# An additive-attention stage on one NeuronCore: from key tile 14 on, the steps follow a table of times, with one exponential for two groups and a fourth numerators' bank

## The chip, the core and the metric

The kernel is one program on one core of a Trainium2 chip. TensorE (PE) multiplies matrices into PSUM, which has eight banks of 128 partitions x 512 float32. VectorE (DVE), ScalarE (ACT) and GpSimd (POOL) work on tiles of 128 partitions; each engine runs its own queue in order, and engines wait for each other by semaphores. The metric is the device time of one execution in microseconds (us), the median of several runs.

## The reference, cut to what matters

The whole model is a selective-scan block (layer 0), then this attention, then a recurrence (layer 1). Only the attention is touched:

```python
t = _to_tokens(x)                      # 4 images, 4096 tokens, 128 channels, float32
t = t + _L1_attn_ref(_ln_t(t), ...)    # _ln_t: layer norm over the channels
...
q = jnp.einsum('bld,ud->blu', x, Wt)   # U = 32
k = jnp.einsum('bld,ud->blu', x, Wx)
beta = jnp.tanh(q[:, :, None, :] + k[:, None, :, :] + bh)
alpha = jnp.einsum('bsju,u->bsj', beta, Wa[:, 0]) + ba[0]
alpha = jnp.tanh(alpha)
alpha = jax.nn.softmax(alpha, axis=-1)
c_r = jnp.einsum('bsj,bjd->bsd', alpha, x)
```

There is a `beta` of 32 values for each of 4 x 4096 x 4096 pairs of query and key, so the tanh can't be formed one by one. The kernel writes a sum of six (or five) tanh terms as one fraction: numerator and denominator are each a sum of 64 (or 32) products of an exponential of the key and an exponential of the query, and such a sum is one matrix product.

## The kernel before

`_bounded` runs three stages: `_layer0`, then `_rational` (this attention), then `_chunked` (the recurrence). `_rational` works through 32 blocks: four images `b`, each with eight blocks `s` of 512 queries. For one block the keys come in 32 tiles `jt` of 128, so `A[:, jt, :]` (128 keys x 512 queries) is the score of one step. `F` holds the keys' exponentials, `E` the queries', `cE` the queries' with the weights of the numerators.

The 32 units are split into three groups: "A" (two fractions, each a product over 64 rows, on partitions 0 to 63 and 64 to 127), "B1" (two over 32 rows, partitions 0 to 31 and 32 to 63) and "B2" (two over 32 rows, partitions 64 to 95 and 96 to 127). A step does for each group:

- `lower`: two matmuls into a tile `pd` of two PSUM banks, the denominators (line 1212). `pd` has two buffers.
- `upper`: two matmuls into two tiles `pn` of one bank each, the numerators (line 1212 too). `pn` has three buffers; one more bank, `ct`, is for the weighted sum and for small products.
- `inverse`: 1/denominator as Ln (line 1231, PSUM to SBUF) and Exp with scale -1 (line 1232, in place), both on ACT over 128x1024.
- `times`: two DVE multiplications of the inverse by the numerators (line 1227), which free the `pn` banks.

POOL adds the three groups: B1 to A on line 1346, B2 to A on line 1333 (below a1 and a2). DVE then adds the two halves into `A[:, jt, :]` on line 1343 (below f); f is the one DVE operation of a step with both inputs in SBUF. The results `ra` have three buffers, `rb` four.

A stage is scheduled by hand: each engine's queue has the order in which the Python code issues. In one step of the loop (line 1323) PE does dA(j), nB2(j-1), dB1(j), nA(j), dB2(j), nB1(j), where d are lower and n upper products; ACT does Ln and Exp of A, then of B1, then of B2; DVE does xB2(j-1), xA(j), xB1(j), f(j-1), where x is `times`; POOL does a2(j-1), a1(j).

After the 32 steps comes the tail (line 1380): ACT runs tanh and exp over `A` in four parts. Meanwhile DVE does step 0 of the next block with reciprocals of its own (`direct`, lines 1239 and 1240) and f of that step (line 1396); before that it forms the next `cE` (`weigh`, line 1200), on which the first numerators of the next block wait. PE sums `ct` over key tiles 0 to 19 in the tail (`weighted`, line 1357).

The rest is put between the steps of the next block, by the dictionary `between`, after the step whose number is the key: the last twelve `weighted` at 2 to 13; at `CLOSE_AT` the closing of the block before: `ct` copied to SBUF (1249), one matmul for the denominator (1253), four reciprocals of 128x128 that read it in PSUM (1258), one matmul for the numerator (1262), a multiplication (1263), POOL's addition to `xr` (1264) and the store; at `NORM_AT` the layer norm of 512 tokens of the next image (centre, square, rate, scale; lines 1149 to 1164), in the blocks of the first three images; at `QUERIES_AT` the two matmuls, exponentials and maxima for the next block's `E` (line 1194). At the first block of an image eight `turn` (transposes into `xT`) are put in too.

Of the kernel before, what the change touches and what calls it, by code (L numbers as in the profile page):

```python
# [15 lines left out]
P = 128  # L16
B = 4
# [25 lines left out]
CLOSE_AT = (14, 16, 17, 18, 19, 20, 22)  # L43
NORM_AT = (15, 17, 19, 20)
QUERIES_AT = (24, 26)
# [1000 lines left out]
def _rational(ctx, tc, k, x1, x2, top, Wt, Wx, bh, Wa, ba):  # L1046
# [15 lines left out]
    rb = ctx.enter_context(tc.tile_pool(name="nrb", bufs=4))  # L1062
    psD = ctx.enter_context(tc.tile_pool(name="npsD", bufs=2, space=PSUM))
    psN = ctx.enter_context(tc.tile_pool(name="npsN", bufs=3, space=PSUM))
    psW = ctx.enter_context(tc.tile_pool(name="npsW", bufs=1, space=PSUM))
# [6 lines left out]

    def pn():
        return psN.tile([P, QB], F32, name="pn", tag="pn")

    def pw():
        return psW.tile([P, QB], F32, name="ct", tag="ct")
# [65 lines left out]
    def norm_steps(xn, cols, alloc):  # L1143
# [10 lines left out]
        def square():  # L1154
            held["sq"] = rb.tile([P, CH], F32, name="sq", tag="rb")[:, 0:n]
            nc.scalar.activation(held["sq"], xc, AF.Square)
# [37 lines left out]
    def queries(E, xn, s, i):  # L1194
        exponent(pw(), w_q, xn[:, s * QB : (s + 1) * QB], i, E[:, i, :])
# [33 lines left out]
    def inverse(d, pool, tag):  # L1229
        r = pool.tile([P, 2, QB], F32, name=tag, tag=tag)  # L1230
        nc.scalar.activation(r, d, AF.Ln, scale=LOWER)  # L1231
        nc.scalar.activation(r, r, AF.Exp, scale=-1.0)  # L1232
        return r

    def direct(d, ns, pool, tag):

        r = pool.tile([P, 2, QB], F32, name=tag, tag=tag)
# [3 lines left out]
        return r  # L1241

    def closing(b, s, ct, xr, parts):
# [7 lines left out]
        def denominators():  # L1251
            held["den"] = pw()
            nc.tensor.matmul(held["den"], den_w, held["ct"], start=True, stop=True)
            held["rec"] = one.tile([P, QB], F32, name="rec")

        def invert(i):
            cols = slice(i * QB // parts, (i + 1) * QB // parts)
            nc.vector.reciprocal(held["rec"][:, cols], held["den"][:, cols])

        def end():  # L1260
            num = pw()
# [32 lines left out]
    between = {}  # L1294
    for c in range(1, nq):
        for i in range(2):
            between.setdefault(2 * c - 2 + i, []).append(lambda c=c, i=i, xn=xn: keys(F, xn, c, pw(), i))
    for c in range(nq):
        between.setdefault(16 + c, []).append(lambda c=c, xn=xn: turn(xT, xn, c))
    for b in range(B):  # L1300
        upcoming = None
        for s in range(nq):
# [4 lines left out]
            if b + 1 < B:  # L1307
# [4 lines left out]
                for at, go in zip(NORM_AT, norm_steps(upcoming, blocks[s], pn)):  # L1312
                    between.setdefault(at, []).append(go)
            if more:
                E_next = two.tile([P, 2, QB], F32, name="E")
                of = upcoming if turned else xn
                for i in range(2):
                    between.setdefault(QUERIES_AT[i], []).append(
                        lambda i=i, s=s, of=of, E_next=E_next: queries(E_next, of, (s + 1) % nq, i)
                    )  # L1320
            ln_exp()
            late = None
            for jt in range(start, JT + 1):
                if jt < JT:
                    dA = lower("A", F, jt, E) if jt > start else first[0]
                if late is not None:
                    pj, rA_, rB2_ = late
                    nB2 = upper("B2", F, pj, cE)
                if jt < JT:
                    dB1 = lower("B1", F, jt, E) if jt > start else first[1]  # L1330
                if late is not None:
                    times(rB2_, nB2)
                    nc.gpsimd.tensor_tensor(rA_, rA_, rB2_, ALU.add)  # L1333
                if jt < JT:
                    nA = upper("A", F, jt, cE)
                    rA = inverse(dA, ra, "ra")
                    times(rA, nA)
                    dB2 = lower("B2", F, jt, E)
                    nB1 = upper("B1", F, jt, cE)
# [322 lines left out]
```

## Time and profile before

| what | us |
|---|---|
| median of 3 runs (from 11648.04 to 11656.42) | 11649.02 |
| the profiled execution's own time | 11654.41 |
| its span, first to last instruction | 11652.7 |
| PE busy, of the span | 10307.6 (88%) |
| ACT busy | 9520.9 (82%) |
| DVE busy | 8997.6 (77%) |
| POOL busy | 8625.1 (74%) |
| the attention's groups: Ln of `rb` (1231), x1986 | 2007.6 |
| Exp of `rb` (1232), x1986 | 2099.6 |
| Ln of `ra` (1231), x993 | 1008.7 |
| Exp of `ra` (1232), x993 | 1049.6 |

The page divides the span into 40 slices, and gives for each engine a digit of busy tenths. The attention takes the slices from the fourteenth on, up to nearly the last. The page's groups give the count and the mean time of one instruction; the timeline gives each instruction's start, its duration, and in brackets how long its engine had been idle before it and what ended that. Instructions of one kind that follow each other are merged in the timeline (x2, x4). A float32 matmul is two passes, each with its weight load.

### The profile page before, as it was taken

Reading aid. Unit: us, or ns where it says so; the run is one execution under the profiler, and the core shown is the slowest. Engines: PE = TensorE matmul, PEld = TensorE weight load, DVE = VectorE, ACT = ScalarE, POOL = GpSimd, SP = SyncE. Lnnn points to the kernel's source line nnn. Section 1 sums busy time; section 2 is a strip of 40 time slices with the busy share of each in tenths; the row PEclk is TensorE's granted clock in tenths of the full one; section 3 lists DMA queues with packets and bytes.
Section 4 is the critical chain, followed back from the end, with each engine's and each line's share of the span. In section 5 each row is a group of like instructions: output and inputs, shape, how many; then the busy total and the mean of one; then the engine's idle time right before and its main releaser. Section 6 shows DMA issues by size and latency. Waiting matters only on the chain.

```text
span 11652.7 us, 111820 instructions
## 1 busy us (share of the span) xinstructions
PE 10307.6 (88%) x36210; PEld 3184.3 (27%) x36210; DVE 8997.6 (77%) x10066; ACT 9520.9 (82%) x10209; POOL 8625.1 (74%) x3703
## 2 busy tenths in 40 slices
PE   6787787778777699999999999999999999999997
PEld 2121121122111133333333333333333333333334
DVE  4998899889889677777777777777777777777773
ACT  3566556656655599999999999999999999999996
POOL 3999889889889677767766776767677767776773
PEclk8898898889888799999999999999999999999998
DMA  4888778778778300000000000000000000000001
GB/s 118 189 182 194 171 177 193 170 182 190 179 171 186 79 1 3 6 3 3 6 3 3 3 6 3 3 3 6 3 3 3 6 2 3 3 4 3 2 3 60
DMA packets 225332, 737.77 MB, mean 63 GB/s; under 512 B 41104, under 2 KB 41936, under 8 KB 223712
## 3 DMA queue, kind: packets, MB, share of 16 engines
q1 hardware_dynamic: 221760, 729.96, 26.5%
q8 instruction: 286, 4.69, 0.2%
q14 instruction: 310, 2.54, 0.1%
q10 hardware_dynamic: 2976, 0.58, 0.0%
HBM read 612.95 MB, written 117.44 MB: 63 GB/s over the span
## 4 chain that ended last, share of the span: by engine, by line
PE 50%; ACT 9%; DVE 4%; issue 3%; POOL 0%; DMA 0%; DVEq 0%; POOLq 0%; SPq 0%; ACTq 0%
PE pn L1212 26%; PE pd L1212 16%; PE ct L1357 4%; ACT A L1381 3%; ACT A L1382 2%; DVE rb L1227 2%; ACT rb L1231 1%; ACT rb L1232 1%; PE ct L1134 1%; ACT ra L1231 1%; DVE rb L1239 1%; PE vy L1556 0%; DVE A L1343 0%; PE pn L56 0%; PE ct L1262 0%
## 5 line engine op out<-in xcount | busy, mean ns | idle before, releaser
L1212 PE MATMUL pn<-cE,F 32*128 32x512 f32 (+1 forms) x12288 | 4728.8, 650 | 196.6 <-DVE rb L1227 88.5
L1227 DVE TENSOR_TENSOR rb<-rb,pn 128x512 f32<-128x512 f32 x3972 | 2544.5, 682 | 1310.9 <-PE pd L1212 684.9
L1212 PE MATMUL pd<-E,F 32*128 32x512 f32 (+1 forms) x12288 | 3478.0, 648 | 20.9 <-DVE ra L1239 15.7
L1346 POOL TENSOR_TENSOR ra<-ra,rb 128x1024 f32<-128x1024 f32 x993 | 2634.5, 2653 | 957.2 <-DVE rb L1227 956.9
L1333 POOL TENSOR_TENSOR ra<-ra,rb 128x1024 f32<-128x1024 f32 x993 | 2346.8, 2363 | 409.0 <-DVE rb L1227 348.4
L626 POOL TENSOR_TENSOR dBu<-dtdu,bbcc 128x1024 f32<-128x1024 f32 x1024 | 2398.3, 2368 | 216.9 <-DMA dtdu<-ddd 155.5
L1232 ACT ACTIVATE rb<-rb 128x1024 f32<-128x1024 f32 x1986 | 2099.6, 1057 | 62.8
L1212 PEld LDWEIGHTS pn<-cE,F 32*128 32x128 f32 (+1 forms) x12288 | 1418.0, 185 | 2574.8 <-DVE rb L1227 1066.6
L1231 ACT ACTIVATE rb<-pd 128x1024 f32<-128x1024 f32 x1986 | 2007.6, 1011 | 89.9 <-PE pn L1212 75.2
L668 PE MATMUL py<-h,gather 128*32 128x512 f32 x4096 | 1297.9, 699 | 477.3 <-POOL h L651 364.5
L1227 DVE TENSOR_TENSOR ra<-ra,pn 128x512 f32<-128x512 f32 x1986 | 1317.9, 684 | 231.4 <-ACT ra L1232 175.6
L1212 PEld LDWEIGHTS pd<-E,F 32*128 32x128 f32 (+1 forms) x12288 | 931.4, 185 | 1638.5 <-issue 693.7
L621 ACT ACTIVATE pa<-dtdu,a_neg 128x1024 f32<-128x1024 f32 x1024 | 1145.3, 1119 | 53.1 <-DVE h L641 32.1
L651 POOL TENSOR_TENSOR h<-h,bbcc 128x1024 f32<-128x1024 f32 x384 | 912.0, 2375 | 346.2 <-ACT carry L649 338.5
L641 DVE TENSOR_TENSOR_SCAN pa<-pa,carry,dBu 128x1024 f32<-128x1024 f32 x480 | 1124.7, 2343 | 23.1 <-ACT pa L621 11.3
L1232 ACT ACTIVATE ra<-ra 128x1024 f32<-128x1024 f32 x993 | 1049.6, 1057 | 31.4
L1357 PE MATMUL ct<-A,xT 128*128 128x512 f32 x2048 | 1050.9, 641 | 8.2 <-ACT A L1382 8.2
L1231 ACT ACTIVATE ra<-pd 128x1024 f32<-128x1024 f32 x993 | 1008.7, 1016 | 60.0 <-PE pd L1212 26.5
L649 ACT COPY carry<-pa 128x1 f32<-128x1 f32 x640 | 102.4, 160 | 1043.7 <-DVE h L648 1041.9
L1343 DVE TENSOR_TENSOR A<-ra 128x512 f32<-128x512 f32 x993 | 745.0, 750 | 116.3 <-POOL ra L1333 116.0
L648 DVE TENSOR_TENSOR h<-pa,bbcc 128x1024 f32<-128x1024 f32 x640 | 784.1, 1225 | 59.0 <-PE py L668 0.9
L641 DVE TENSOR_TENSOR_SCAN h<-pa,carry,dBu 128x1024 f32<-128x1024 f32 x288 | 675.0, 2344 | 171.1 <-PE py L668 148.2
(291 smaller groups left out, 8731.3 us busy)
## 6 DMA issues: line engine op xcount, KB each, us to landing
bbcc<-bcd SPq DMA_DIRECT2D x1024, 256.0 KB, 6.9
dtdu<-ddd SPq DMA_DIRECT2D x1024, 256.0 KB, 7.1
ddd<-dd SPq DMA_DIRECT2D x64, 1024.0 KB, 5.1
src<-src SPq DMA_DIRECT2D x64, 512.0 KB, 8.3
xs<-in_x_dram SPq DMA_DIRECT2D x16, 512.0 KB, 7.5
src<-xs SPq DMA_DIRECT2D x16, 512.0 KB, 3.0
bcd<-bc SPq DMA_DIRECT2D x64, 128.0 KB, 2.0
src<-xsT SPq DMA_DIRECT2D x16, 512.0 KB, 5.4
```

Of the source, the lines that this page charges most:

```text
L621: nc.scalar.activation(dA, its[m].DT[r][:, 0, :], AF.Exp, scale=a)
L626: nc.gpsimd.tensor_tensor(dBu, its[m].DT[r][:, 1, :], its[m].BC[q][:, 0, :], ALU.mult)
L641: nc.vector.tensor_tensor_scan(to[:, step], dA[:, step], live.pop(("dBu", u))[:, step], 0.0 if m % nch == 0 else its[m - 1].carry[:, col : ...
L651: nc.gpsimd.tensor_tensor(h, h, cc, ALU.mult)
L668: nc.tensor.matmul(it.y[to, c], gather, live["h", v][:, c], start=False, stop=(q == QS - 1))
L1212: nc.tensor.matmul(ps[a], F[lo:hi, i, jt * P : (jt + 1) * P], side[lo:hi, i, :], start=True, stop=True)
L1227: nc.vector.tensor_tensor(r[:, a, :], r[:, a, :], ns[a], ALU.mult)
L1231: nc.scalar.activation(r, d, AF.Ln, scale=LOWER)
L1232: nc.scalar.activation(r, r, AF.Exp, scale=-1.0)
L1333: nc.gpsimd.tensor_tensor(rA_, rA_, rB2_, ALU.add)
L1346: nc.gpsimd.tensor_tensor(rA, rA, rB1, ALU.add)
L1357: nc.tensor.matmul(ct, xT[:, jt, :], A[:, jt, :], start=(jt == 0), stop=(jt == JT - 1))
```

## The change

1. The loop over `jt` is replaced by `steps`, which gives for each tile a list of (time, function). The lists of all tiles and what stood in `between` are sorted by time, and issued in that order. A table says at what time, counted in steps from the tile's own number, each operation stands. Tiles below `LATE` = 14 have a table that gives the old order. Tiles from 14 on have another.
2. From tile 14 on the Ln of B1 and of B2 write the two halves of one tile of 128x2048 and one Exp does both. In the new order ACT does lnA, lnB1, exA, lnB2, exB; PE does nB1(j-1), dB2(j), nB2(j-1), dA(j+1), nA(j), dB1(j+1); DVE does xB1(j-1), f(j-2), xB2(j-1), xA(j); POOL does a1(j-1), a2(j-1).
3. `rb` becomes three buffers of 128x2048 (each has room for B1 and B2 of a step) where there were four of 128x1024.
4. The four single banks are now tiles `pn0` to `pn3`. `pn()` takes them in turn: three of them up to time 13.95, four from there to the end of the steps, where the bank of `ct` has been copied out. `pw()`, which the weighted sum uses, is always `pn3`.
5. The closing moves to the times 13.95 to 18.9. The denominators are copied from PSUM to `rec` in SBUF (one DVE instruction more for each block), and the reciprocals read them there. Its matmuls and those of the queries take a bank by `pn()`.
6. The norm moves from after the steps 15, 17, 19, 20 to the times 19.9, 20.95, 21.95, 23.95; its squares share the buffer of `rec`. The queries stay after step 24 and 26 by their number (24.9 and 26.9), the `weighted` come a step earlier (1.9 to 12.9).

```diff
-CLOSE_AT = (14, 16, 17, 18, 19, 20, 22)
-NORM_AT = (15, 17, 19, 20)
-QUERIES_AT = (24, 26)
+LATE = 14
+CLOSE_AT = (13.95, 15.9, 16.4, 16.9, 17.4, 17.9, 18.9)
+NORM_AT = (19.9, 20.95, 21.95, 23.95)
+QUERIES_AT = (24.9, 26.9)
+EARLY_STEPS = dict(
+    dA=0.00, dB1=0.10, nA=0.20, lnA=0.21, exA=0.22, xA=0.23, dB2=0.30, nB1=0.31, lnB1=0.40, exB1=0.41,
+    xB1=0.42, a1=0.44, lnB2=0.50, exB2=0.51, nB2=1.05, xB2=1.12, a2=1.13, f=1.43,
+)
+LATE_STEPS = dict(
+    dA=-0.44, dB1=-0.23, lnA=-0.12, lnB1=-0.04, exA=0.26, dB2=0.37, lnB2=0.50, nA=0.74, xA=0.81, exB=0.84,
+    nB1=1.11, xB1=1.38, nB2=1.42, xB2=1.49, a1=1.75, a2=1.88, f=2.46,
+)
...
-    rb = ctx.enter_context(tc.tile_pool(name="nrb", bufs=4))
+    rb = ctx.enter_context(tc.tile_pool(name="nrb", bufs=3))
...
-    psN = ctx.enter_context(tc.tile_pool(name="npsN", bufs=3, space=PSUM))
-    psW = ctx.enter_context(tc.tile_pool(name="npsW", bufs=1, space=PSUM))
+    psN = ctx.enter_context(tc.tile_pool(name="npsN", bufs=1, space=PSUM))
...
+    turns = {"taken": 0, "banks": 3}
     def pn():
-        return psN.tile([P, QB], F32, name="pn", tag="pn")
+        i = turns["taken"] % turns["banks"]
+        turns["taken"] += 1
+        return psN.tile([P, QB], F32, name=f"pn{i}", tag=f"pn{i}")
     def pw():
-        return psW.tile([P, QB], F32, name="ct", tag="ct")
+        return psN.tile([P, QB], F32, name="pn3", tag="pn3")
...
+    def four():
+        return rb.tile([P, 4, QB], F32, name="rb", tag="rb")
+    def steps(jt, F, E, cE, A, first):
+        h = {}
+        when = EARLY_STEPS if jt < LATE else LATE_STEPS
+        go = {}
+        def halves(u):
+            if "rb" not in h:
+                h["rb"] = four()
+            return h["rb"][:, 0:2, :] if u == "B1" else h["rb"][:, 2:4, :]
...
+        go["lnB1"] = lambda: log(halves("B1"), h["dB1"])
+        go["lnB2"] = lambda: log(halves("B2"), h["dB2"])
+        if jt >= LATE:
+            go["exB"] = lambda: exp(h["rb"])
+        else:
+            go["exB1"] = lambda: exp(halves("B1"))
+            go["exB2"] = lambda: exp(halves("B2"))
...
+        go["a1"] = lambda: nc.gpsimd.tensor_tensor(h["ra"], h["ra"], halves("B1"), ALU.add)
+        go["a2"] = lambda: nc.gpsimd.tensor_tensor(h["ra"], h["ra"], halves("B2"), ALU.add)
+        go["f"] = lambda: nc.vector.tensor_tensor(A[:, jt, :], h["ra"][:, 0, :], h["ra"][:, 1, :], ALU.add)
+        return [(jt + when[name], f) for name, f in go.items()]
...
         def denominators():
-            held["den"] = pw()
-            nc.tensor.matmul(held["den"], den_w, held["ct"], start=True, stop=True)
-            held["rec"] = one.tile([P, QB], F32, name="rec")
+            den = pn()
+            nc.tensor.matmul(den, den_w, held["ct"], start=True, stop=True)
+            held["rec"] = one.tile([P, QB], F32, name="rec", tag="rec")
+            nc.vector.tensor_copy(held["rec"], den)
...
-            nc.vector.reciprocal(held["rec"][:, cols], held["den"][:, cols])
+            nc.vector.reciprocal(held["rec"][:, cols], held["rec"][:, cols])
...
+            between.append((CLOSE_AT[0], lambda: turns.update(banks=4)))
+            for jt in range(start, JT):
+                between += steps(jt, F, E, cE, A, first if jt == start else None)
+            for _, go in sorted(between, key=lambda e: e[0]):
+                go()
+            turns["banks"] = 3
+            between = []
...
-                    between[2 + i] = [lambda jt=jt, weighted=weighted: weighted(jt)]
+                    between.append((1.9 + i, lambda jt=jt, weighted=weighted: weighted(jt)))
```

## The prediction

> **What bounds the kernel now.** I first read the slices of busy time: from the fourteenth on (the attention) PE and ACT are both at nine tenths or more, and PE's digit may hold waiting inside matmuls.
>
> ```profile
> PE   6787787778777699999999999999999999999997
> DVE  4998899889889677777777777777777777777773
> ACT  3566556656655599999999999999999999999996
> POOL 3999889889889677767766776767677767776773
> ```
>
> So I read the timeline of ACT alone in a late, undisturbed step.
>
> ```profile
> 7450.81 0.58 ACT L1135 ACTIVATE E<-ct 128x512 f32<-128x512 f32 x1
> 7451.29 1.01 ACT L1231 ACTIVATE ra<-pd 128x1024 f32<-128x1024 f32 x1
> ...
> 7457.30 1.01 ACT L1231 ACTIVATE ra<-pd 128x1024 f32<-128x1024 f32 x1
> 7458.34 1.06 ACT L1232 ACTIVATE ra<-ra 128x1024 f32<-128x1024 f32 x1
> 7459.31 1.01 ACT L1231 ACTIVATE rb<-pd 128x1024 f32<-128x1024 f32 x1
> ...
> 7463.31 1.01 ACT L1231 ACTIVATE ra<-pd 128x1024 f32<-128x1024 f32 x1
> ...
> 7484.76 1.91 ACT L1382 ACTIVATE A<-A 128x2048 f32<-128x2048 f32 x1
> 7486.58 3.69 ACT L1381 ACTIVATE A<-A,b_a 128x4096 f32<-128x4096 f32 x1
> ```
>
> ACT sets the pace: 7463.31 - 7457.30 = 6.01 us a step with no gap. An Exp begins 1.04 after the Ln that it needs; an instruction that needs nothing of the one before starts about 0.10 before that one's end: 0.96 after an Exp, 0.48 after the 0.58 us E.
>
> Then the timelines of DVE and POOL, for what breaks this pace.
>
> ```profile
> 7456.63 0.69 DVE L1343 TENSOR_TENSOR A<-ra 128x512 f32<-128x512 f32 x1
> 7456.86 2.68 POOL L1346 TENSOR_TENSOR ra<-ra,rb 128x1024 f32<-128x1024 f32 x1 [1.02 <-DVE rb L1227]
> ...
> 7418.11 2.36 POOL L1346 TENSOR_TENSOR ra<-ra,rb 128x1024 f32<-128x1024 f32 x1
> 7418.20 2.83 DVE L1343 TENSOR_TENSOR A<-ra 128x512 f32<-128x512 f32 x1 [0.42 <-POOL ra L1333]
> ```
>
> Where f starts first, it takes 0.69 and a1 waits some 0.3 inside its 2.68. Where a1 is 0.09 ahead, f lasts until a1 is over: 2.83. This happens once in 30 of the 32 blocks, after the norm's or the closing's extra POOL work. The step around it lasts 7.8 to 11.0 us instead of 6.0, 3.5 more in the mean (starts of lnA in blocks 1 to 23).
>
> Last the tail.
>
> ```profile
> 7486.01 0.69 DVE L1343 TENSOR_TENSOR A<-ra 128x512 f32<-128x512 f32 x1 [3.28 <-POOL ra L1333]
> ...
> 7511.16 0.69 DVE L1240 SCALAR_TENSOR_TENSOR rb<-rb,pn 128x512 f32<-128x512 f32 x1
> ...
> 7511.85 1.28 ACT L1068 ACT_TABLE_LOAD   x1
> ```
>
> DVE's reciprocals and ACT's exponentials end together, at 7511.85: a DVE that starts later ends the tail later.
>
> **What the change saves.** In the new order only exB follows directly on what it needs. Starts to starts: lnA 0.91, lnB1 0.91 (1.01 less 0.10), exA 0.96, lnB2 1.04, exB 1.82 (the 128x2048 Exp at 7484.76): 5.64 us a step. From lnA(14) to the load of the tanh's table that is 17 x 5.64 + 5.73 (the last, with exB to its end) = 101.6, and ACT's other work there: two E at 0.48, and with a norm 0.52 + 1.24. So 104.3 with norm, 102.6 without. The same stretch before, read off the lnA starts of each block: 116.6 in the first, 115.4 (mean of the next 23), 112.6 (last eight). The saving, if nothing waits, is 12.3 + 23 x 11.1 + 8 x 10.0 = 348 us. The upper bound of a step: both Ln still cost their whole 1.01, 5.84, which takes back 0.2 x 17 x 32 = 109. I take 5.64, since the E and Exp rows show the 0.10 on both of ACT's sources.
>
> **Can PE follow?** A pair of matmuls alone takes 1.06 (7455.22 to 7456.28). No row shows two pairs on the same partitions in one shape; sixteen passes of `ct` take 7.13, thus 0.43 for each after the first, and the next pair 0.86. The lower bound is 0.86, the upper 1.06; I take 0.86, the row of unbroken matmuls. PE's chain in a step: lnA(j) ends (1.06 with the semaphore), dB2 and nB2 1.92, dA and nA 1.92, dB1 1.06 and 0.11 to be visible: 6.07 after lnA(j), where lnB1(j+1) is due at 6.55. So PE has 0.48 to spare (with 1.06 each: 0.1). DVE needs 4.3 and POOL 2.68 + 2.36 = 5.04 of 5.64. POOL's spare time is 0.6 where it was 0.96, and f(j-1) has only some 0.3 between its data and a1(j).
>
> **What it pays.** (a) The closing, 31 blocks. The reciprocals at 16.4 and 17.4 stand between xB1 and f. A reciprocal holds DVE 0.87; a1 starts 0.15 after xB1's end, so f finds POOL at work and waits: it ends 0.15 + 2.36 + 0.56 = 3.07 after xB1. `ra` has three buffers, so lnA(17) waits for f(14): following the queues from step 14, xB1(15) ends 9.53 after lnA(15) (the denominators' matmul is ahead of nB1), f(14) 12.6 after it, and lnA(17) was due at 11.28: 1.4 late. The second time DVE is already behind, and lnA(18) is 1.9 late. The numerators' matmul costs 0.4 more. 3.7 x 31 = 115; bounds 0.5 (f is not held) and 2 x 3.5 + 0.5 a block. The extra copy (0.68) fits where DVE waits for nB1.
> (b) The queries: PE reaches the matmul 0.32 after lnA and its result is there at 1.48; ACT wants it at 0.91. 0.57 x 2 x 31 = 35 (0 to 60). Before, no E waited. The norm's rate likewise 0.57, the centre 0.2: 24 x 0.77 = 18.
> (c) The scale on POOL (1.27) doesn't fit into 0.6: bounds 0 and 3.5, I take 1.0 x 24 = 24. Eight turns at four blocks, 0 to 1.06 each (one matmul's place): 0.3 x 32 = 10.
> (d) The tail. After lnA(31) no dA or dB1 follows, so PE and DVE run ahead: xB1(31) ends at 7.07 (exB at 5.73), a1(31) could start at 7.22, but POOL has a2(30) until 7.79. It goes straight on with a1(31); f(30), which needs a2(30), comes 0.09 later and is held to 10.7. xB2(31) ends at 11.9, a2(31) at 14.4, f(31) begins at 14.5: 8.8 after the table load, where it was 7486.01 - 7481.43 = 4.6. `weigh` and the reciprocals stand behind f on DVE, so the next block's f(0), xA(1), nB1(1) and dA(2) come 4.2 late, and lnA(2), which had 1.1 to spare, 3.1. 31 x 3.1 = 96 (2.0 a block if f is not held, 4.2 at most).
> The `weighted` a step earlier, the table for tiles below 14 and the buffers of `rb` I cost at nothing: PE's order there is as before, and a2 of three steps ago is long over; if not, lnB1 would wait for POOL.
>
> 115 + 35 + 18 + 24 + 10 + 96 = 298 against 348: 50 us saved, less about 4 for PE's half clock after longer waits (1.44 for a pair after 2.07 us of idling at 6734.01). 11654.4 - 46 = 11608, made against the profiled execution, which is 5.4 above the median.
>
> For the reciprocals from SBUF the trace has no row. The Trainium skill, "SBUF — State Buffer", section "Who interferes with whom", says that a VectorE instruction with at most one SBUF input outside the two-port modes does not contend with GpSimd: by it they hold nobody up themselves and the sum stays. If they did contend as f does, four holds of up to 2.36 would make (a) up to 9 us a block. No run here shows which.
>
> **The rivals.** *The port decides (slower).* Once more in each block f comes behind POOL, at the closing's addition to `xr` (18.9) or at the scale. For it: 0.3 of slack, and 30 such cases in the old, wider steps; against: ACT's other waits there give POOL time. Price 3.5 x 31 = 108: 11716. It decides from 1.5 us a block. *f is never held (faster).* POOL's queue might let DVE in between: (a) falls to 0.5, (d) to 2.0: 99 + 34 less, 11475. Against it stand the thirty rows of 2.83. *ACT gains only the merged Exp*: 5.84 a step, 11717. *PE's pairs take 1.06 each*: every inserted matmul then costs 0.4 to 0.6 more, 2.6 a block with norm and 1.7 without (75), 13 for turns, 19 in the tail: 11715.
>
> **How the numbers follow.** The forecast has 0.42, with its own range 11560 to 11660; the port 0.25, f never held 0.17, the last two 0.08 each. 0.2% (about what can be told from no change) is 23 us. Of the forecast 0.28 lies below 11626 and 0.12 within; with the third case faster is 0.45, same 0.12, slower 0.43. The range 11485 to 11740 leaves out half of the fast case and the upper ends of the slow ones.
>
> **What would show it.** lnA to lnA 5.64 in steps 28 to 30; 0.91 from lnA to lnB1; f of 2 us or more at the steps 16 and 17 and at the end of each block, over 90 in all; f(31) 8 to 9 us after the table load; E 0.5 late; the first step of a block 9 us long instead of 6.0. If ACT waits for PE in undisturbed steps, or if f is held in most steps, the sum is wrong from its base.

## The result and the profile after

The changed kernel takes **11739.04 us** (median of 4 runs, 11735.44 to 11741.83), the kernel before 11649.98 beside it (median of 4). The ratio is 1.0075 with a 95% interval of 1.0058 to 1.0093: slower by some 89 us, where 46 us faster was forecast. The profiled execution took 11738.35, with a span of 11736.6.

The slices of busy time of the changed kernel, one row for each engine:

```profile
PE   6787787778777699999999999999999999999997
...
DVE  4998899889889577777777777777777777777773
ACT  3566556656655599999989999989999999999996
POOL 3999789889889577677757776767677666666673
```

PE is as before; ACT, which set the pace, has an 8 here and there, and DVE's digits tell nothing. So the steps have to be looked at. The timeline of ACT in a late step where nothing waits (start, duration, instruction):

```profile
6555.13 1.01 ACT L1249 ACTIVATE ra<-pd 128x1024 f32<-128x1024 f32 x1
6556.03 1.02 ACT L1249 ACTIVATE rb<-pd 128x1024 f32<-128x1024 f32 x1
6556.94 1.06 ACT L1252 ACTIVATE ra<-ra 128x1024 f32<-128x1024 f32 x1
6557.89 1.02 ACT L1249 ACTIVATE rb<-pd 128x1024 f32<-128x1024 f32 x1
6558.94 1.91 ACT L1252 ACTIVATE rb<-rb 128x2048 f32<-128x2048 f32 x1
6560.76 1.00 ACT L1249 ACTIVATE ra<-pd 128x1024 f32<-128x1024 f32 x1
```

A step is 6560.76 - 6555.13 = 5.63 us (6.01 before, 5.64 forecast), and each start-to-start is as the prediction had it: 0.90, 0.91, 0.95, 1.05, 1.82. The change does what it says. The loss lies elsewhere. Two groups of the page of the changed kernel (instruction, count | busy us, mean ns | idle before it, and what ended most of that):

```profile
L1302 POOL TENSOR_TENSOR ra<-ra,rb 128x1024 f32<-128x1024 f32 x993 | 2608.1, 2627 | 883.6 <-DVE rb L1246 779.9
...
L1304 DVE TENSOR_TENSOR A<-ra 128x512 f32<-128x512 f32 x993 | 993.8, 1001 | 237.2 <-POOL ra L1303 229.2
```

f costs 1.00 us in the mean; before it was 0.75, and a free one is 0.69. In the trace 151 f last 2 us or more (they are called held below), against 30 before, and 31 more last about 1.4.

From the starts of lnA and of the tanh's table load, the attention can be cut into the stretches of the prediction (blocks 1 to 31, us per block; "forecast" is the prediction's own terms put together: 104.3 + 3.7 + 2 x 0.57 + 0.77 + 1.0 + 0.3 for a block with norm, 102.6 + 3.7 + 1.14 + 0.3 for one without):

| stretch | before | forecast | measured | off, over all blocks |
|---|---|---|---|---|
| lnA(1) to lnA(14) | 81.9 | 85.0 | 85.8 | +27 |
| lnA(14) to the table load, blocks 1 to 23 | 115.4 | 111.2 | 112.1 | +21 |
| the same, blocks 24 to 31 (last image, no norm) | 112.6 | 107.7 | **116.1** | +67 |
| table load to the next lnA(1), sum | 1005.9 | 1005.9 | 1022.0 | +16 |

The sum is 131, and the forecast was off by 11738.35 - 11608 = 130. Half of it is in eight blocks. The first stretch is longer in its first step alone, lnA(1) to lnA(2), which is 10.1 us where it was 6.0.

The timeline of DVE and POOL in the changed kernel shows two blocks at the same place, tile 18's f: first a block with norm, then one of the last image (in brackets the idle time before, and who ended it):

```profile
6500.10 2.37 POOL L1303 TENSOR_TENSOR ra<-ra,rb 128x1024 f32<-128x1024 f32 x1
6500.28 0.69 DVE L1168 TENSOR_TENSOR xn<-xn,pn 128x512 f32<-128x512 f32 x1
6501.40 1.29 DVE L1246 TENSOR_TENSOR rb<-rb,pn 128x512 f32<-128x512 f32 x2 [0.43 <-PE pd L1231]
6502.60 0.69 DVE L1304 TENSOR_TENSOR A<-ra 128x512 f32<-128x512 f32 x1
6502.83 2.69 POOL L1302 TENSOR_TENSOR ra<-ra,rb 128x1024 f32<-128x1024 f32 x1 [0.37 <-DVE rb L1246]
...
10229.94 2.37 POOL L1303 TENSOR_TENSOR ra<-ra,rb 128x1024 f32<-128x1024 f32 x1
10230.09 1.29 DVE L1246 TENSOR_TENSOR rb<-rb,pn 128x512 f32<-128x512 f32 x2
10232.25 2.37 POOL L1302 TENSOR_TENSOR ra<-ra,rb 128x1024 f32<-128x1024 f32 x1
10232.34 2.83 DVE L1304 TENSOR_TENSOR A<-ra 128x512 f32<-128x512 f32 x1 [0.97 <-POOL ra L1303]
```

In both f needs the result of a2 (L1303), and stands behind xB1 (L1246 on `rb`) in DVE's queue. In the first block the norm's subtraction (L1168) makes xB1 end at 6502.69, 0.22 after a2, so POOL has to pause before a1 (L1302), and f goes first. In the second, xB1 has ended at 10231.38, long before a2 does; POOL goes from a2 straight on to a1, and f comes 0.09 too late and is held until a1 is over. So the question at each step is whether a1's data are there before a2 ends.

What follows a hold can cost more than the hold. The same block of the last image on ACT, and then four stretches of it (start:end and length; busy time and instructions of PE, PE's weight loads, DVE, ACT and POOL; then the clock granted to PE, 1.00 being full speed; last the DMA):

```profile
10235.26 1.02 ACT L1249 ACTIVATE ra<-pd 128x1024 f32<-128x1024 f32 x1 [0.81 <-DVE A L1304]
10241.90 1.02 ACT L1249 ACTIVATE ra<-pd 128x1024 f32<-128x1024 f32 x1 [0.90 <-DVE A L1304]
10244.98 1.02 ACT L1249 ACTIVATE rb<-pd 128x1024 f32<-128x1024 f32 x1 [2.06 <-PE pd L1231]
...
10259.08 1.02 ACT L1249 ACTIVATE rb<-pd 128x1024 f32<-128x1024 f32 x1 [2.41 <-PE pd L1231]
```

```profile
10228.00:10235.00 7.00, 6.75 (x30) 2.45 (x28) 5.96 (x7) 6.42 (x6) 6.54 (x3) 1.00 0.21 73
10235.00:10242.00 7.00, 6.18 (x20) 2.44 (x20) 6.85 (x9) 5.81 (x6) 4.72 (x2) 0.72 0.00 0
10242.00:10246.00 4.00, 3.97 (x20) 1.90 (x16) 2.31 (x5) 1.94 (x3) 2.36 (x1) 0.63 0.00 0
10256.00:10260.00 4.00, 3.90 (x20) 1.21 (x16) 1.87 (x4) 1.59 (x3) 2.35 (x1) 0.67 0.00 0
```

The holds themselves make lnA of tiles 21 and 22 wait 0.81 and 0.90. Behind the first one PE, which needs a bank that xB2 frees, is idle for 1.07; then its granted clock falls, and lnB1 of tiles 22 and 24 wait 2.06 and 2.41 for PE's lower products. The steps 20 to 24 of this block are 6.9 us longer than five of 5.63: 1.7 of that are the two waits for f, 4.5 the two for PE.

### The profile page after: what moved, and what is told of

Its sections match the earlier page's. It is cut to its first block, busy times and chain, and to the rows that moved or that the text cites. A ratio compares the mean times of both kernels' runs of the same rounds, so it can differ in the third digit from the quotient of the medians.

```text
span 11736.6 us, 108835 instructions
## 1 busy us (share of the span) xinstructions
PE 10251.2 (87%) x36210; PEld 3386.1 (29%) x36210; DVE 9219.5 (79%) x10098; ACT 9338.0 (80%) x9633; POOL 8596.2 (73%) x3703
## 4 chain that ended last, share of the span: by engine, by line
PE 46%; DVE 10%; POOL 5%; ACT 3%; issue 2%; DMA 0%; POOLq 0%; DVEq 0%; SPq 0%; ACTq 0%
PE pn L1231 21%; PE pd L1231 17%; PE pn L1399 5%; DVE rb L1257 3%; DVE rb L1246 2%; POOL ra L1303 2%; DVE A L1304 2%; POOL ra L1302 2%; DVE ra L1257 2%; ACT rb L1249 1%; ACT ra L1249 1%; PE pn L1150 1%; DVE rb L1258 1%; PE vy L1599 0%; POOL ra L1421 0%
## 5 line engine op out<-in xcount | busy, mean ns | idle before, releaser
L1231 PE MATMUL pn<-cE,F 32*128 32x512 f32 (+1 forms) x12288 | 3905.1, 643 | 250.2 <-DVE cE L1219 175.7
L1246 DVE TENSOR_TENSOR rb<-rb,pn 128x512 f32<-128x512 f32 x3972 | 2546.8, 681 | 1006.2 <-PE pd L1231 570.8
L1302 POOL TENSOR_TENSOR ra<-ra,rb 128x1024 f32<-128x1024 f32 x993 | 2608.1, 2627 | 883.6 <-DVE rb L1246 779.9
L1303 POOL TENSOR_TENSOR ra<-ra,rb 128x1024 f32<-128x1024 f32 x993 | 2346.7, 2363 | 592.3 <-DVE rb L1246 551.1
L1252 ACT ACTIVATE rb<-rb 128x1024 f32<-128x1024 f32 (+1 forms) x1410 | 1982.4, 1406 | 44.8
L1231 PEld LDWEIGHTS pn<-cE,F 32*128 32x128 f32 (+1 forms) x12288 | 1355.6, 191 | 2112.7 <-issue 843.2
L1246 DVE TENSOR_TENSOR ra<-ra,pn 128x512 f32<-128x512 f32 x1986 | 1304.0, 682 | 187.2 <-PE pn L1231 168.9
L1304 DVE TENSOR_TENSOR A<-ra 128x512 f32<-128x512 f32 x993 | 993.8, 1001 | 237.2 <-POOL ra L1303 229.2
L1399 PE MATMUL pn<-A,xT 128*128 128x512 f32 x2048 | 1048.5, 640 | 4.5 <-ACT A L1427 4.5
```

The source lines that it names most:

```text
L1231: nc.tensor.matmul(ps[a], F[lo:hi, i, jt * P : (jt + 1) * P], side[lo:hi, i, :], start=True, stop=True)
L1246: nc.vector.tensor_tensor(r[:, a, :], r[:, a, :], ns[a], ALU.mult)
L1302: go["a1"] = lambda: nc.gpsimd.tensor_tensor(h["ra"], h["ra"], halves("B1"), ALU.add)
L1303: go["a2"] = lambda: nc.gpsimd.tensor_tensor(h["ra"], h["ra"], halves("B2"), ALU.add)
L1304: go["f"] = lambda: nc.vector.tensor_tensor(A[:, jt, :], h["ra"][:, 0, :], h["ra"][:, 1, :], ALU.add)
L1399: nc.tensor.matmul(ct, xT[:, jt, :], A[:, jt, :], start=(jt == 0), stop=(jt == JT - 1))
```

## The experiments

All times are single runs unless an interval is given. The kernel before took 11647 to 11655 (medians) beside them, so that differences under 10 us are not read from the totals, and small ones only where steps of the trace show them.

**1. The closing's reciprocals behind f**

```diff
-CLOSE_AT = (13.95, 15.9, 16.4, 16.9, 17.4, 17.9, 18.9)
+CLOSE_AT = (13.95, 15.9, 16.47, 16.9, 17.47, 17.9, 18.9)
```

> The changed kernel with two of the four reciprocals at 16.47 and 17.47 instead of 16.4 and 17.4, so that they stand behind f and not between xB1 and f. If it is the port (f comes behind a1 because a reciprocal holds VectorE 0.87 us): the two held f (2.26 us each) become 0.69, the steps 16 to 18 fall from 7.03 + 7.43 + 6.8 to about 6.2 + 6.0 + 6.0, 3.2 us in each of 31 blocks, and the time from 11739 to about 11640. If it is the matmul of the denominators and the banks: within 20 us of 11739.

Measured: 11627.02, 112 less than the changed kernel. The steps 16 to 18 go from about 7.04, 7.43 and 6.80 to 5.63 each in most blocks (block 26 among them). So moving two reciprocals by 0.07 of a step turns the change from a loss into a small gain. 97 f of 2 us or more remain of 151: further holds come later in the block.

**2. The old order in tiles 30 and 31**

```diff
-        when = EARLY_STEPS if jt < LATE else LATE_STEPS
+        late = LATE <= jt < JT - 2
+        when = LATE_STEPS if late else EARLY_STEPS
...
-        if jt >= LATE:
+        if late:
```

> The changed kernel with the old order for the tiles 30 and 31 of every block. If the end of the steps delays the tail (xB1(31), then two additions on GpSimd and a held f(30) ahead of f(31) and weigh): f(31) is back at 4.6 us after the table load, the first step of a block at 6.0 to 6.3 instead of 10.1, 4.0 x 31 = 124 less; two steps of 6.0 instead of 5.62 cost 0.8 x 31 = 24; together about 11640. If the first step is long for another reason (the weighted sums a step earlier, the three banks in turn): it stays at 10.1 and the time is about 11760.

Measured: 11861.92, slower by 123. The theory missed: the change of order costs 3 us a block by itself (the step from tile 30 to 31 takes 7.6 to 9.4 us in all blocks but the last), f at the end is still held, f(31) begins 9.7 us after the table load and not earlier, and the first step is 11 us. It says nothing on what makes the first step long.

**3. No addition to `xr`** (the addition of the attention's part to `xr` is left out)

```diff
-            nc.gpsimd.tensor_tensor(xr, xr, held["rec"], ALU.add)
```

> The changed kernel without GpSimd's addition of the attention's result to xr (left out: the output lacks the attention's part). If that 1.27 us is what makes GpSimd late in the last image's blocks, the held f at 41.9, 48.5 and 62 us after lnA(14) are gone there, lnA(14) to the table load falls from 116.1 to about 111.5 in these 8 blocks, and the time by 35 to 45 us, to about 11700. If these blocks are slow because the norm's work is missing (GpSimd has no pause): no change beyond 10 us.

Measured: 11716.34, 23 less. The f of 1.4 us are gone, but in the blocks 25 to 31 a hold begins anyway, 41 to 44 us after lnA(14); in four of them five holds follow each other at 6.64 us a step, in the last block ten. The late part of the last image's blocks falls only from 116.1 to 114.5, where 111.5 was expected. So the addition to `xr`, the rival's place, is not what starts these holds, and one hold is followed by the next. In block 26 PE's waits between these five are 0.35 to 0.76, its granted clock stays at 1.00 (10222 to 10253), and no hold costs more than 1.0 us.

**4. f as a sum with one input**

```diff
-        go["f"] = lambda: nc.vector.tensor_tensor(A[:, jt, :], h["ra"][:, 0, :], h["ra"][:, 1, :], ALU.add)
+        go["f"] = lambda: nc.vector.tensor_reduce(A[:, jt, :], h["ra"].rearrange("p a q -> p q a"), AX.X, ALU.add)
```

> The changed kernel with f as one reduction over the two halves (one SBUF input, the same sum) instead of an addition of two SBUF inputs. If the port decides: no f is held though each takes about 1.1 us instead of 0.69, a1 takes 2.36 instead of 2.63, lnA(14) to the table load is 104 to 107 in all blocks instead of 112 to 116, the first step of a block 8 to 8.5 instead of 10.1; 7 x 23 + 10 x 8 + 1.8 x 31 = about 300 less, 11440. If the waits come from TensorE and the banks: within 50 us of 11739, or above, since VectorE works 0.4 us more in each step.

Measured: 11548.42, 191 less than the changed kernel and 102 less than before. The timeline of this kernel at a place like the held f above:

```profile
10094.73 2.37 POOL L1302 TENSOR_TENSOR ra<-ra,rb 128x1024 f32<-128x1024 f32 x1
10094.81 1.24 DVE L1304 TENSOR_REDUCE A<-ra 128x512 f32<-128x1024 f32 x1 [0.47 <-POOL ra L1303]
```

a1 is ahead by 0.08 as it was by 0.09 there, and f takes 1.24 and not 2.83. None of the 993 f lasts over 1.31. POOL gains too: its a1 fall from 2.63 to 2.36 us in the mean, since f no longer holds them. The gain is less than expected: the first step falls only to 8.7, and of the steps 16 to 22 with closing and norm most still take 6.0 to 7.0.

**5. The same in the kernel before** (the same edit of its f)

> The kernel before, with its f as the one-input sum instead of the two-input addition; nothing else is changed. The trace of before has 30 f that are held for 2.83 us, one in a block, each about 2.1 us longer than a free one. If the held f is a defect of the meeting of f and the additions of POOL in either order of work, then before can gain at most about 30 x 3.5 = 105 us, and probably some 30 to 65, because only one step of a block is touched: 11585 to 11620. If the one-input form is worth more than the held f's (something else in it helps, as an earlier release of a buffer), before gains as much as the changed kernel did, about 190: 11460, and then the new order of work is worth nothing by itself. If the 0.54 us more that each f takes on DVE is on the path in the old order, the time rises by up to 0.54 x 992 = 535 us.

Measured: 11613.07, 34 less than before. So the new order with the one-input f (11548) beats the old order with it by 65 us: the change is worth something by itself, and f's holds took that and more.

**6. f(31) behind the first reciprocals of the tail**

```diff
+        if jt == JT - 1:
+            last.append(go.pop("f"))
...
                     ahead(0)
+                    last.pop()()
```

> The changed kernel, with f of key tile 31 issued after the first pair of reciprocals of the next block's tile 0 instead of before them; it is needed only by the last part of the tanh, 19.6 us after the table load. In the changed kernel f(31) ends DVE's tail at 9.4 us after the table load and everything behind it on DVE (E's two scalings, six reciprocals of 4.06 us with their multiplications) starts 4.2 us later than before; the first step of a block is 10.1 us for 6.0. If that is what lengthens the first step, E is scaled at about 6.2, the reciprocals begin at about 7.0, the first step falls to 6.5 to 7.5 and the time by 31 x 2.6 to 3.6 = 80 to 110 us: 11630 to 11660. If the first step is long for another reason (the order of the numerators' banks in the first steps, or the shared buffer of four), it stays at about 10 us and the time at 11735.

Measured: 11735.68, no difference. But the edit did not do what it should. DVE's tail in this kernel (L1219 is E's scaling, twice; L1305 is a2(31)):

```profile
6339.57 2.98 DVE L1219 TENSOR_SCALAR cE<-E,c_n 128x512 f32<-128x512 f32 x2
...
6339.79 2.48 POOL L1305 TENSOR_TENSOR ra<-ra,rb 128x1024 f32<-128x1024 f32 x1 [1.89 <-DVE rb L1246]
...
6342.47 3.34 DVE L1257 RECIPROCAL ra<-pd 128x512 f32<-128x512 f32 x1
```

The two scalings take 0.88 in the changed kernel. Here they meet POOL, and the second is held to 2.58. The last reciprocal begins 29.94 us after the table load instead of 30.45, and the first step falls by as much, from 10.1 to 9.6 in the median. That is too little to tell what makes it long; run 9 tries it again.

**7. Two exponentials in the late steps**

```diff
-            go["exB"] = lambda: exp(h["rb"])
+            go["exB"] = lambda: (exp(halves("B1")), exp(halves("B2")))
```

> The changed kernel, with the one exponential for two groups in tiles 14 on given as two, at the same place in the order. If the merged instruction is worth its own difference (1.92 us for 2 x 1.06 with a start-to-start gap of about 0.96, so 0.1 us) and ACT sets the steady step, a steady step goes from 5.62 to about 5.73, and a block, of whose 18 late steps some 9 are steady, loses 1.0 to 2.0 us: 32 to 64 us more, 11770 to 11800. If the saving of the steady step (6.0 to 5.62) comes from the merge as a whole, a steady step is back at 6.0 and the time at 11840 to 11950. If f's hold decides the late part rather than ACT, the longer step leaves POOL more room, f is held less often, and the time stays or falls, down to 11700.

Measured: 11715.72, 23 less. A steady step in this kernel's timeline of ACT:

```profile
6546.48 1.03 ACT L1249 ACTIVATE ra<-pd 128x1024 f32<-128x1024 f32 x1
...
6549.23 1.05 ACT L1249 ACTIVATE rb<-pd 128x1024 f32<-128x1024 f32 x1
6550.14 2.04 ACT L1252 ACTIVATE rb<-rb 128x1024 f32<-128x1024 f32 x2
6552.03 1.06 ACT L1249 ACTIVATE ra<-pd 128x1024 f32<-128x1024 f32 x1
```

A step is 5.55 us, 0.07 shorter than with one exponential. From lnB2 to the next lnA it is 0.91 + 1.89 = 2.80, with the merge 1.05 + 1.82 = 2.87: the merged instruction must wait for the logarithm just before it, whereas exB1 needs nothing of it. The gain of the steady step is the order's, and the merge takes some of it back. The theory on record expected 5.73 and missed; 23 us is what a total can just tell, the step is plain.

**8. Three banks in the late steps**

```diff
-            between.append((CLOSE_AT[0], lambda: turns.update(banks=4)))
+            between.append((CLOSE_AT[0], lambda: turns.update(banks=3)))
```

> The changed kernel, with the numerators of tiles 14 on taking turns over three banks of PSUM, as in tiles 0 to 13, and not over four. If the fourth bank is needed for the new order (four pairs' worth of numerators lie between the earliest matmul and the last multiplication), PE waits for a bank in each step and a steady step goes from 5.62 to 6.0 or more: 18 x 32 x 0.4 = 230 us or more, 11970 and up. If three would do, the time stays at 11735 within 15, and the fourth bank's part in the change is nothing.

Measured: 11991.59, 253 more. The late part takes 121 us a block for 112 to 116. Steady steps lose less than expected (5.63 to 5.80), the steps with the closing, norm and queries more (up to 10.3). The fourth bank is needed.

**9. The last two f on POOL**

```diff
-            nc.vector.tensor_scalar(cE[:, i, :], E[:, i, :], c_n[:, i : i + 1], None, ALU.mult)
+            to, of = (t[:, i, :].rearrange("p (u v) -> p v u", v=2) for t in (cE, E))
+            nc.vector.tensor_scalar(to, of, c_n[:, i : i + 1], None, ALU.mult)
...
+        if jt >= JT - 2:
+            go["f"] = lambda: nc.gpsimd.tensor_tensor(A[:, jt, :], h["ra"][:, 0, :], h["ra"][:, 1, :], ALU.add)
```

> The changed kernel, with f of key tiles 30 and 31 issued on POOL (after a2 of its tile) and the two scalings of E read and written in steps of two elements, so that DVE's tail waits for POOL at no place. In the trace of the changed kernel DVE's first reciprocal of the tail begins 10.15 us after the table load (before 5.97) and the last one 30.45 (before 26.27). The experiment on f(31) moved it only by 0.5 us to 29.94, because the second scaling of E, 0.48 us alone, then lay beside a2(31) and took 2.58 us; so it said nothing on the first step. Theory (the first step is long because DVE begins its tail late): the first reciprocal begins at about 5, the last at about 25, the first step of a block falls from 10.1 to 6.0 to 6.3, and the time by 31 x 3.8 to 4.1 = 118 to 127 us: 11610 to 11625. Rival (the first step is long for the order of the banks or the buffers of the early steps): it stays near 10 us and the time near 11735. If steps of two elements do not take the scaling out of POOL's way, the first reciprocal begins at about 7.5 and the first step is 7 to 7.5: 11645 to 11660.

Measured: 11667.44, 72 less. The scaling in steps of two is still held (2.59 beside a POOL addition), but the first reciprocal begins 6.23 us after the table load and the last 26.99, nearly as before. The first step falls from 10.1 to 7.7 (median). So DVE's late start is most of the long first step, as far as this edit tells. lnB1(1) begins 34.5 us after the table load in the median (33.7 before, 36.1 in the changed kernel). Where it is on time, the first step is 6.2 in one block (2) and 7.2 in another (5), so something else has a part too.

**10 and 11. One-input f, reciprocals behind f and the last two f on POOL; then with two exponentials** (the edits of 4, 1 and 9; of 4, 1, 9 and 7)

> Three parts together: f as a sum of one input, the closing's reciprocals behind f, the last two f of a block on POOL with the scaling in steps of two. From the run with f of one input alone (11548): its first step of a block was 8.73, which should fall to 6.0 to 6.3 (31 x 2.4 to 2.7 = 75 to 85 us), and its steps 16 to 18, 5.96 and 6.35 for 5.62, should fall by 1.0 a block (31): 11430 to 11445. If f was not the whole of what is held (a rival: POOL and DVE still meet elsewhere, or PE is what the remaining long steps wait for), the parts do not add up and the time stays at 11480 or above.

> The run before it, with two exponentials in place of the one for two groups. In the changed kernel the merged instruction begins 1.06 us after the logarithm that it needs, where an instruction that needs nothing of the one before begins 0.94 after it, and with two exponentials a steady step took 5.55 us and not 5.62. If ACT's chain decides in the steady steps, of which a block has here some 12 of 18 in tiles 14 on, two exponentials gain 0.07 x 12 x 32 = 27 us, up to 0.07 x 18 x 32 = 40: 11390 to 11415, and the merge is a loss by itself. If PE or POOL (5.04 us of work in a step) decides at this pace, the time is the same within 15.

Measured: 11478.99, ratio to before 0.9853 (0.9836 to 0.9869), and 11467.18, ratio 0.9843 (0.9826 to 0.9859). No f is held in either. The parts do not add up fully: 11430 to 11445 was expected of the first. Its first steps are 6.2 to 8.2 and not 6.0 to 6.3, and the steps 17 to 22 of a block with norm stay at 5.9 to 7.0. The first is at the rival's 11480. The second is 12 us lower, and each of its four runs lies below each of the first's, but the theory had 27 to 40 and the rival the same within 15. The steady steps are 5.62 and 5.55, so ACT still decides in these; the last image's late parts got longer with it (105.9 to 107.2), and why is open.

**12. More work for DVE in the last image**

```diff
+        def linger():
+            nc.vector.reciprocal(held["rec"][:, 0:192], held["rec"][:, 0:192])
...
+                if b == B - 1:
+                    between += [(at, todo[-1]) for at in (19.9, 20.9, 21.9)]
```

> The changed kernel, with three useless reciprocals of 192 columns (from and to SBUF, about 1.3 us each by the rows of 0.94 for 128 and 3.35 for 512 columns) on DVE at 19.9, 20.9 and 21.9 in blocks 25 to 31, which have no norm; the result is not touched. In the changed kernel's trace a block of the norm and one of the last image run alike up to tile 18; then the norm's subtraction (0.69 at 39.57 us after lnA(14)) makes xB1 end at 41.98, a1 begins at 42.13 behind f at 41.90, and f is not held; in the last image xB1 ends at 40.92, POOL goes from a2 straight on to a1 at 41.80, and f comes 0.09 us too late and is held for 2.83. Theory (f is held because a1's data are there before a2 ends, so that POOL does not pause): more work on DVE ahead of xB1 takes the holds at 41.9, 48.5 and 62.1 us away, the late part of these blocks falls from 116.1 to 112 to 114, and the time by 7 x 2 to 4 = 14 to 28 us although DVE does more. Rival (the holds come from DVE and POOL both having too much to do): three holds or more stay, the late part rises by 1 to 4 us to 117 to 120, and the time by 7 to 28 us.

Measured: 11704.44, **35 less although DVE does more**. The timeline of POOL and DVE in this kernel, at tile 18's f of block 26, and then near the end of the last block:

```profile
10223.42 2.36 POOL L1303 TENSOR_TENSOR ra<-ra,rb 128x1024 f32<-128x1024 f32 x1
10223.43 1.34 DVE L1333 RECIPROCAL rec<-rec 128x192 f32<-128x192 f32 x1
10224.70 1.21 DVE L1246 TENSOR_TENSOR rb<-rb,pn 128x512 f32<-128x512 f32 x2
10225.83 0.68 DVE L1304 TENSOR_TENSOR A<-ra 128x512 f32<-128x512 f32 x1
10226.06 2.70 POOL L1302 TENSOR_TENSOR ra<-ra,rb 128x1024 f32<-128x1024 f32 x1 [0.27 <-ACT rb L1249]
...
11391.86 2.36 POOL L1302 TENSOR_TENSOR ra<-ra,rb 128x1024 f32<-128x1024 f32 x1
11391.87 2.90 DVE L1304 TENSOR_TENSOR A<-ra 128x512 f32<-128x512 f32 x1 [0.16 <-POOL ra L1303]
11396.11 2.37 POOL L1303 TENSOR_TENSOR ra<-ra,rb 128x1024 f32<-128x1024 f32 x1 [1.89 <-DVE rb L1246]
11398.50 2.37 POOL L1302 TENSOR_TENSOR ra<-ra,rb 128x1024 f32<-128x1024 f32 x1
11398.52 2.90 DVE L1304 TENSOR_TENSOR A<-ra 128x512 f32<-128x512 f32 x1 [0.16 <-POOL ra L1303]
```

With the reciprocal, xB1 ends later than a2, POOL pauses, and f goes first: four steps of 5.63 follow where 5.63, 6.53, 6.63 and 7.81 stood, and PE's granted clock is 1.00 over all four (10222 to 10245). The late part of the last image's blocks falls from 116.1 to 112.3. Not all holds are gone: from 59.7 us after lnA(14) on, behind the last of the added reciprocals, two follow each other in block 26. The last rows show how a hold feeds itself. f is held by a1; xB2 stands behind f, so a2 waits 1.89 for it; meanwhile DVE works off xA and the next xB1, and a1's data are there when a2 ends. In the last block, which has no queries to break this, the step is 6.64 us until the end, ten holds in a row.

**13 and 14. The weighted sums a step later; and all parts together** (14 has the edits of run 11 too)

```diff
-                    between.append((1.9 + i, lambda jt=jt, weighted=weighted: weighted(jt)))
+                    between.append((2.9 + i, lambda jt=jt, weighted=weighted: weighted(jt)))
```

> The changed kernel, with the weighted sums of tiles 20 to 31 given at 2.9 and on instead of 1.9 and on, each one step later, where they stood before the change. The prediction had costed their move at nothing. In the run with the last two f on POOL the logarithm lnB1(1) began on time, 33.8 us after the table load (before 33.7), and still the first step was 7.3 to 8: PE has one weighted matmul, 1.06 us, right ahead of the lower sums of A(2), for which lnA(2) waits. Theory: the first step of a block falls from 10.1 to 9.0 and the time by 31 x 1.06 = 33 us: 11705. Rival (the 1.06 us lie beside DVE's lateness and only that decides): the first step stays at 10.1 and the time at 11738.

> The run with f of one input, the closing's reciprocals behind f, the last two f on POOL and two exponentials (11467), with the weighted sums a step later too. There the first step of a block is 6.95 in the median and 6.2 to 8.2 in all (before 6.02). Theory (the weighted matmul ahead of A(2) is what is left): first step 6.0 to 6.3, a gain of 0.7 to 1.06 a block, 22 to 33 us: 11434 to 11445. Rival (PE's late end of the sixteen weighted sums in the tail decides): the same within 10 us.

Measured: 11710.03 for 13, 29 less than the changed kernel. The first step is 9.02 for 10.09, so this step's theory holds. Some is given back at step 14, where the last of the weighted sums now stands at the change of order: it takes 6.08 or 6.92 (mean 6.40) for 5.62. Run 14 is 11485.16, ratio 0.9853 (0.9837 to 0.9870), no gain over run 11: 14 of its 31 first steps are 6.0, but its late parts are longer by 33 us in all, 18 of them at step 14 as in run 13. That theory missed. What PE does in a first step, in the timeline of the changed kernel:

```profile
6382.70 1.13 PE L1399 MATMUL pn<-A,xT 128*128 128x512 f32 x2
6383.76 1.13 PE L1231 MATMUL pd<-E,F 64*128 64x512 f32 x4
...
6385.00 1.02 ACT L1249 ACTIVATE ra<-pd 128x1024 f32<-128x1024 f32 x1 [1.47 <-PE pd L1231]
```

The weighted sum of tile 20 (L1399) delays A(2)'s lower sums by 6383.76 - 6382.70 = 1.06, and lnA(2) waits for these.

## Why the prediction was wrong, point by point

- **ACT sets the pace, and a late step is 5.64**: right, 5.63. The remark that only exB follows directly on what it needs was right as well, and its consequence was not drawn: two exponentials would be faster (5.55, run 7).
- **PE can follow**: right for steady steps, also for those of 5.55 in run 7.
- **(a) The closing, 3.7 us a block for two held f**: right in mechanism. The three steps lose 4.4 (7.04 + 7.43 + 6.80 - 3 x 5.62), and run 1 takes this away. But the third step's 1.2 is not the numerators' matmul, for which 0.4 was added: lnB1(18) waits 1.19 for PE, whose granted clock is 0.54 just before (10214 to 10218, block 26). The reciprocals from SBUF, whose price no row had shown, are not held: all 124 of 128 columns take about 0.94, and no a2 of POOL takes more than 2.38 either.
- **(b) The queries, 0.57 each**: in most blocks the second costs this (6.70 - 5.62 = 0.48 for E and 0.60), and the first nothing beside E's 0.48 (6.11). Too high by about 0.5 a block. The step ahead of the first, 24, loses 1.2 in blocks with norm, but not by the queries: in block 15 lnB1(24) waits 1.08 for PE, whose granted clock is 0.50 there (7669 to 7671).
- **(c) The scale on POOL, 1.0 a block, and nothing for the addition to `xr`**: this is the step that failed. The prediction took the midst of a range, as if a hold were an event with a price. The runs showed that it is nearer to a state: after a hold POOL has the next a1 ready, and the next f is held too (two in a row in the changed kernel's block 26, up to ten in run 3 and in run 12), until something makes xB1 late. Blocks with norm have such work and end 0.9 over the forecast, blocks without have none and end 8.4 over it: 67 of the 130 us. Run 12 takes 3.8 of the 8.4 away, and with no f held at all (run 4) these blocks take 107.6. The rival *the port decides* had the right mechanism and sign. That its 11716 came near is in part luck: it priced one more hold of 3.5 in each block, at the addition to `xr`, which run 3 cleared, or at the scale, while the holds of 2.8 us stand elsewhere, one in most blocks with norm (47 us after lnA(14), the scale is at 65) and several in each of the others. "ACT's other waits there give POOL time" was held against it without regard to the eight blocks that have no such waits.
- **"Less about 4 for PE's half clock"**: too small, and a part of the same failed step. In the steps 20 to 24 of block 26 ACT waits 4.5 us for PE at a lowered clock, in most other blocks of the last image about as much; in the kernel before, all its waits for PE in the late part of block 26 are 2.2. In run 12 the two long waits are gone from block 26. Five holds in run 3 left the clock at 1.00, so not each hold brings this; no run changes the clock alone, and how much of the 67 is its part stays open.
- **(d) The tail, 3.1 us a block**: right. f(31) begins 8.75 us after the table load (8.8 forecast). Of the 4.07 us in the first step, 1.07 are the weighted sum's (run 13), so 3.0 are left for DVE's lateness; run 9, which takes that away, gained 2.4 in the median.
- **"The `weighted` a step earlier ... I cost at nothing: PE's order there is as before"**: wrong, 1.07 x 31 = 33 us in the first steps, and 29 in run 13's total. The order of the tile's own operations is as before, but a matmul that stood behind step 2's work now stands ahead of A(2), just where lnA(2) had 1.1 to spare, and (d) had used this up.
- **Turned blocks**: the 16 us by which the tails grew had no term (a turned block's tail is 55.2 to 55.4 us for 48.8 to 50.5 before). In run 9, with DVE's tail nearly on time, 12 of the 16 are gone, so most of it belongs to (d).
- **The signs**: 5.64, 0.91, f(31), 0.48 of wait before the second E of a block and "over 90" long f all came; the first step was 10.1 for 9. That f is held in most steps, the sign named for a sum wrong from its base, came in the last block alone (11 of its 18 late f, and one more of 1.41).
- **The other rivals**: *ACT gains only the merged Exp* falls with the step of 5.63, *f is never held* with the 151 held ones. *PE's pairs take 1.06 each* falls for the steady step: there a group's lower and upper products take 1.92, 1.79 and 1.92 together (PE's starts at 6552.48, 6554.40, 6556.19 and 6558.11), and not 2.12.

Open is why the first steps of runs 10, 11 and 14 differ from block to block (6.0 to 8.5), and where the 15 us of run 14's late parts that don't stand at step 14 come from.

## What to carry to other kernels

When two engines share something and the loser waits for the winner's whole instruction, ask of each step not what a lost race costs but whether losing it makes the next one lost too: compare the data that the winner needs next with the moment it gets free, and do this for every kind of block. Before reordering around such a meeting, change the form of the instruction that loses; here one line was worth 191 us, and the whole change, with that line on both sides, 65. Look also at what stands idle behind a hold: here PE's granted clock fell after some of them, and ACT then waited longer for PE than for the held instruction. An instruction that is moved by one step costs nothing only if what now stands behind it has slack left after all other terms.

## What the runs showed of the hardware

- The form decides who meets POOL. With POOL's addition ahead by less than 0.1 us, a DVE addition with two SBUF inputs took 2.83 us and a reduction of the same data as one input 1.24 (0.69 and 1.23 alone). A scaling (`tensor_scalar`, 0.48 alone) took 2.58, although it has one tensor as input; with elements in steps of two it took 0.48 alone as well and up to 2.59 beside POOL.
- The Trainium skill, "SBUF — State Buffer", section "Who interferes with whom", says that on trn2 `tensor_reduce` never contends with GpSimd, and lists `tensor_scalar` among the operations that can take the shared pair of ports. Runs 4, 6 and 9 agree with both.
- PE's granted clock fell from 1.00 to 0.72 and 0.63 in the stretches behind an idle time of 1.07 us (block 26), and a pair of products began 1.87 after the one before (10239.14 to 10241.01) where it was 0.96 (6553.44 to 6554.40). Four idle times of 0.35 to 0.76, a step apart, left it at 1.00 (run 3).
- On ACT an instruction that needs the result of the one before it starts about 1.05 us after that one's start, one that does not 0.91 (logarithms of 128x1024). Merging two exponentials into one that has to wait cost 0.07 us a step more than it saved.
